# First layer of a two-layer kernel: decays and a norm factor spread over partitions by a trip through DRAM in place of transposes on TensorE

## The chip, the cores and the metric

The kernel runs on one core of a Trainium2 chip. The metric is the device time of one execution in microseconds (us); lower is better. The core has TensorE (PE in the profile, with PEld for its weight loads), VectorE (DVE), ScalarE (ACT), GpSimd (POOL) and SyncE (SP), which issues the DMAs here; SPq is SP's queue.

## What is computed

The input is 16 sequences of 512 tokens with 128 features. Both layers normalise the input, run two branches on it and add both to the residual. Cut to the part that the change touches, layer 0 is:

```
xn     = (x - mean) / sqrt(var + 1e-5)                  # layer norm, all tokens
# branch 1: a gated linear recurrence
xi, z  = split(xn @ W_in)
proj   = xi @ W_xp
delta  = softplus(proj[..., :1])                         # one number for each token
B, C   = proj[..., 1:65] @ W_B,  proj[..., 65:] @ W_C
A_bar  = exp(-exp(A_log) * delta)                        # one decay for each token, the same for all 256 channels
h_t    = A_bar_t * h_(t-1) + (B * xi)_t                  # scan over the tokens of a sequence
y      = ((C * h + D * xi) * silu(z)) @ W_out
# branch 2: eight experts, the best one for each token
top1   = argmax(xn @ Wg.T)
xhat   = layernorm(xn)                                   # a second norm, of xn
y2     = W2[top1] @ gelu(W1[top1] @ (xhat * scale + bias) + b1) + b2
x      = x + y + y2
```

Layer 1 is an attention of 16 heads with decays and level weights over dyadic segments of each sequence, plus a gated cell that runs over the 16 sequences one after another (the state of sequence b feeds sequence b + 1).

## The kernel before

**Stages.** The loop over i from -2 to 18 is layer 0, one sequence (called a batch below) for each step, with its stages spread over neighbouring steps: `norm0_stats(i+2)`, `norm0(i+2)` and `route(i+2)`, then `step_size(i+1)`, `decay_rows(i+1)` and `route2(i+1)`, then `mixers(i)`, `residual(i-1)`, `hand_over(i-2)` and `cell_step(i-3)`. The second loop, over 17 steps, is layer 1: `states`, `gates`, `diagonal`, `products`, `upper`, `upper2`, `diagonal2`, `finish`. The first layer-1 batch starts inside the last steps of layer 0. Layer 0 hands its result to layer 1 through DRAM tiles (`d_xt`, `d_xf`, `d_xh`, `d_xl`, and `d_x1`, which the profile shows as `d_x`).

**What sets the order.** No operation goes to the chip where it stands in the code. The class `Plan` records each with its dependences (`record`), prices it (`_price`), and `flush` lists all of them again, engine by engine: at each step the engine that is free earliest takes, among the operations whose inputs are ready by the planner's own clock, the one with the smallest key. The key is the time at which the operation must run for what follows it, plus a random number between -50 and 50 ns (`JIT`, seeded with `SEED`). On TensorE the planner also stays on a bank or on a tile shape where it can, and charges a time for a change of shape (`began += 100.0`). Each engine then runs its list strictly in that order, SyncE with its DMAs too. `record` also decides which earlier operations one depends on: those whose region of a tile it overlaps.

**The tiles that the change touches.** Tokens are laid out as 4 groups of 128 partitions (a column tile of 128 x 4 holds one number for each token). Channel-major work has 128 channels on the partitions and 512 tokens along the row. Two of the per-token numbers are needed channel-major, that is as a row of 512 repeated on all 128 partitions:
- `ab`, the decay, made in `step_size` and needed as `abr` by the two scans of `mixers`;
- `v2`, the factor of the second norm, made in `norm0_stats` and needed in `route` for `xq`, the experts' input.

Before, `spread(col, name)` does this by TensorE: four transposes of 128 x 128, each of one column broadcast along the row, into a PSUM bank. The bank is `par` for the decay, which ScalarE then copies into `abr`; it is `v2r` for the norm factor, which VectorE reads straight out of PSUM in the product `xq = v2r * xr`. `xr` is the transposed `xn`, copied from its bank `pxn` by ScalarE. `split` then makes the two halves `xnh` (rounded) and `xnl` (the rest) for products in three passes; both run on VectorE.

**Names in the profile.** Layer-0 tiles live in memory lent by layer-1 tiles, and the profile shows the lender: `xnh` and `xnl` are `lent_dec_xnh`, `xr` is `lent_ldr_xr`, `abr` is `lent_R_abr` (which also stands for one of the `ge` buffers), `xq` lies in `Gs`, the scans' outputs `hs` in `th_all`, `Gs` and `lent_vbd_x`, and `v2` appears as `v`. All operations carry the line of the statement that issues them, so tiles, not lines, tell them apart.

Of the kernel before, what the change touches and what calls it, by code (L numbers as in the profile page):

```python
# [12 lines left out]
F32 = mybir.dt.float32  # L13
# [3 lines left out]
ALU = mybir.AluOpType  # L17
AX = mybir.AxisListType
PSUM = bass.MemoryType.PSUM
# [3 lines left out]
T = 512  # L23
P = 128
NG = 4
# [21 lines left out]
KEPT = {"tr": 1, "pj": 2, "po": 1, "pg": 1}  # L47
MOST = {"tr": 3, "pj": 4, "po": 2, "pg": 3}

JIT, SEED = 50.0, 4  # L50


BLOCK, FIRST, ASK, LAND, HURRY = 254.25, 192.5, 1400.0, 2450.0, 2.0
# [2 lines left out]
class Plan:  # L56
# [52 lines left out]
    def record(self, eng, name, args, kw):  # L109
        op = Op()  # L110
        op.idx, op.eng, op.name, op.args, op.kw, op.base = len(self.ops), eng, name, args, kw, self.base
        op.deps, op.succ, op.fills, op.uses, op.inst, op.due = set(), [], [], set(), None, 0.0
        op.port = False
        i = op.idx
        aps = [(a, n == 0) for n, a in enumerate(args) if isinstance(a, bass.AP)]
        aps += [(a, False) for a in kw.values() if isinstance(a, bass.AP)]
        for ap, writes in aps:
            t, lo, hi, m = self._region(ap)
            past = self.seen.setdefault(t, [])
            if t in self.ring:  # L120
                op.uses.add(t)
                if not past:
                    op.fills.append(t)
                    self.first[t] = i
                elif self.first[t] != i:
                    op.deps.add(self.first[t])
            keep = []
            for rec in past:
                j, wrote, l, h, q = rec
                hit = l < hi and lo < h and q & m  # L130
                if hit and (writes or wrote) and j != i:
                    op.deps.add(j)
                if not (writes and hit and lo <= l and h <= hi and q | m == m and j != i):
                    keep.append(rec)
            keep.append((i, writes, lo, hi, m))
            self.seen[t] = keep
        if eng == "tensor":
            t = args[0].tensor.name
            if t in self.last_product:
                op.deps.add(self.last_product[t])  # L140
            self.last_product[t] = i
        self._price(op)
        self.ops.append(op)
        return i
# [101 lines left out]
    def flush(self):  # L246
# [79 lines left out]
        while len(order) < len(ops):  # L326
# [13 lines left out]
            while soon[e] and soon[e][0][0] <= now:  # L340
                _, key, i = heapq.heappop(soon[e])
# [5 lines left out]
            if e == "tensor":  # L347

                ahead = HURRY * max(0.0, fetched - now - (BLOCK - count) * 4.2)
                c = min(
                    able,
                    key=lambda c: (
                        c[0] > 1e8 or (
                            strips[ops[c[1]].kw["tile_position"][0] // 32] > strip + 60.0
                            if self._shape(ops[c[1]]) == shape == 2 else ops[c[1]].args[0].tensor.name != bank
                        ),
                        c[0] + 1000.0 * (self._shape(ops[c[1]]) != shape)  # L360
                        + ahead * (self._cols(ops[c[1]].args[0]) <= 64), c,
                    ),
                )
                can[e].remove(c)
                heapq.heapify(can[e])
                o = ops[c[1]]
                for k, n in place.get(o.idx, ()):
                    if not k[0]:
                        banks.pop(0)
                        taken[k] += 1  # L370
                        has[k[1]] += 1
                bank = o.args[0].tensor.name
                w = self._weights(o)
                began = max(now, max(began, o.fed) + (0.0 if w == held else w[2]))
                held = w

                at = max(o.kw["tile_position"]) // 32 if "tile_position" in o.kw else None
                if self._shape(o) != shape:
                    shape = self._shape(o)
                    strips = [0.0] * 4  # L380
                    began += 100.0
                if at is None:
                    strips = [0.0] * 4
                elif any(strips):
                    began = max(o.fed, strip + 17.0, strips[at])

                count += 4 if o.name == "matmul" and o.args[1].dtype == F32 else 2
                if count >= BLOCK:
                    count -= BLOCK
                    began = max(began, fetched)  # L390
                    fetched = max(began + ASK, moved) + LAND

                k = int((began + 100.0) / self.WINDOW)
                warm = columns.get(k - 1, 0.0) >= 3060.0
                o.end = max(began + o.dur * (1.0 if warm else 2.0), now + (22.5 if at is None else 14.5))
                rows = min(P, o.args[1].shape[0])
                part = 1.0 if at is None else 0.25
                columns[k] = columns.get(k, 0.0) + o.dur / 0.4167 * rows / P * part
                if at is not None:
                    strip, strips[at] = began, o.end  # L400
                free[e] = o.end + 2.5
            else:
                c = can[e][0]
                if e == "vector" and pool_end > now:
                    c = min(can[e], key=lambda c: c[0] + ops[c[1]].port * (pool_end - now))
                can[e].remove(c)
                heapq.heapify(can[e])
                o = ops[c[1]]

                if e == "gpsimd":  # L410
                    o.end = pool_end = max(now, port_end) + o.dur
                elif o.port:
                    o.end = port_end = max(now, pool_end) + o.dur
                else:
                    o.end = now + o.dur
                free[e] = o.end
# [40 lines left out]
def two_layer_kernel(ctx: ExitStack, tc: tile.TileContext, a: dict, out: bass.AP):  # L457
# [14 lines left out]
    def bank(name, tag="tr", shape=(P, 512), dt=F32):  # L472
        return nc.bank(ps, shape, dt, tag, name)
# [63 lines left out]
            nc.tensor.transpose(pt[:, g * P : (g + 1) * P], src[:, g, :], ident)  # L537
        return pt

    def spread(col, name):  # L540

        pr = bank(name)
        for g in range(NG):
            nc.tensor.transpose(pr[:, g * P : (g + 1) * P], col[:, g : g + 1].to_broadcast([P, P]), ident)
        return pr


    def handed(name, shape):
# [31 lines left out]
    for u, tag, dt in (  # L580
        ("c2h", "aY", F32R), ("c2l", "aY", F32R), ("xn", "bv", F32), ("c2", "yT", F32), ("tg0", "x1b", F32),
        ("tg1", "ysum", F32), ("x1s", "l0_x1s", F32), ("xr", "ldr", F32),
    ):
        lend(tag, 1, dt, [u])
    for u in ("tg2", "c2"):
        ring.setdefault(u, []).append(bt([P, 1, T], F32, "o", "lent_o_" + u, 2)[:, 0, :])

# [67 lines left out]
    for e in range(8):  # L655
        j = e % 4
# [85 lines left out]
    def norm0_stats(b):  # L742
        n, d = namer(b), S[b]
        xt = d["xt"]
        mv = norm_stats(xt, "la", n)
        rstd = norm_rstd(mv, "la", n)

        v2 = st([P, NG], F32, "v2", n("v2"))
        nc.vector.tensor_tensor(v2, rstd, rstd, op=ALU.mult)
        nc.vector.tensor_tensor(v2, v2, mv[:, :, 1], op=ALU.mult)  # L750
        act(v2, v2, AF.Ln, bias=eps_c)
        act(v2, v2, AF.Exp, scale=-0.5)
        d["norm"] = mv, rstd
        d["v2"] = v2

    def norm0(b):
        n, d = namer(b), S[b]
# [5 lines left out]
    def route(b):  # L763
        n, d = namer(b), S[b]
        pxn = transpose4(d["xn"], n("pxn"))
        xnh = st([P, T], F32R, "xnh", n("xnh"), 3)
        xnl = st([P, T], F32R, "xnl", n("xnl"), 3)
        xr = st([P, T], F32, "xr", n("xr"), 1)
        nc.scalar.copy(xr, pxn)
        split(xnh, xnl, xr)  # L770
        d["xn2"] = (xnh, xnl)
        d["xq"] = xq = st([P, T], F32, "xq", n("xq"))
        nc.vector.tensor_tensor(xq, spread(d["v2"], n("v2r")), xr, op=ALU.mult)

        plg = bank(n("plg"))
        for g in range(NG):
            nc.tensor.matmul(
                plg[32 * g : 32 * g + 32, :P], wlg, xr[:, g * P : (g + 1) * P],
                start=True, stop=True, tile_position=(0, 32 * g),
            )  # L780
        lgs = st([P, P], F32, "lgs", n("lgs"))
        nc.scalar.copy(lgs, plg[:, :P])
        plt = bank(n("plt"))
        nc.tensor.transpose(plt[:, :P], lgs, ident)
        d["lt"] = lt = st([P, NG, 9], F32, "lt", n("lt"))
        nc.vector.tensor_copy(lt, plt[:, :P].rearrange("p (g c) -> p g c", c=32)[:, :, 0:9])
# [37 lines left out]
    def decay_rows(b):  # L824
        n, d = namer(b), S[b]
        d["abr"] = abr = st([P, T], F32, "abr", n("abr"))
        nc.scalar.copy(abr, spread(d["ab"], n("par")))

    def mixers(b):
        n, d = namer(b), S[b]  # L830
# [627 lines left out]
```

## Time and profile before

| | us |
|---|---|
| median of 3 runs | 862.9 (862.58 to 863.74) |
| the profiled execution's own time | 864.26 |
| its span in the profile | 862.4 |
| TensorE (PE) busy | 811.3 (94%) |
| VectorE (DVE) busy | 727.0 (84%) |
| ScalarE (ACT) busy | 630.9 (73%) |
| GpSimd (POOL) busy | 302.7 (35%) |

The span runs from the first to the last instruction; the profiled execution's own time is 1.9 us more. A busy share is the time in which at least one instruction of that engine was in flight, so products that overlap in TensorE's pipeline count once, and the share says nothing of how close the engine is to its rate; the distance from one start to the next does. In a line of the timeline the first two numbers are the start and the duration, in us, of what may be several equal instructions (x4), and a bracket at its end gives the time for which the engine stood idle before it and what ended that. In a group line, the numbers behind the first bar are the busy time of the group in us and the mean of one in ns; behind the second bar is the idle time before it. Line L443 is the planner's single statement that issues everything.

### The profile page before, as it was taken

To read this page: it belongs to the slowest core of one execution; us is meant where nothing else is said; L and a number is where in the kernel's file an instruction comes from. 1 tells how busy PE (TensorE), PEld (TensorE's weight loads), DVE (VectorE), ACT (ScalarE), POOL (GpSimd) and SP (SyncE) were. 2 spreads that over 40 slices of the span, in tenths; PEclk is the share of its full clock that TensorE was granted. 3 is DMA by queue.
4 is the path that set the end of the run, shared out by engine and by line. 5 is a ranking of instruction groups with operands and counts; after the bars stand their busy time and mean duration, and the time that the engine had idled before them with its cause. 6 is when DMAs were issued, how large, how long until landed. Compare 5 with 4: busy or idle time off the path is not lost.

```text
span 862.4 us, 27939 instructions
## 1 busy us (share of the span) xinstructions
PE 811.3 (94%) x11544; PEld 624.6 (72%) x11544; DVE 727.0 (84%) x1841; ACT 630.9 (73%) x1306; POOL 302.7 (35%) x300
## 2 busy tenths in 40 slices
PE   7999999999999888998999999999999999999972
PEld 3778777778778666776787787767777777777752
DVE  5999999999999687668888888878889889888485
ACT  5898889788795777774785786686696687688643
POOL 3423434333434362223225234324333423423311
PEclk8999999999999898999999999999999999999996
DMA  8315223122221234244255345445355344435312
GB/s 211 81 67 170 98 87 111 62 86 74 86 86 62 74 95 154 70 101 114 76 153 138 109 124 139 112 95 151 100 131 143 110 128 121 129 100 136 73 35 62
DMA packets 87539, 91.72 MB, mean 106 GB/s; under 512 B 25893, under 2 KB 63021, under 8 KB 85293
## 3 DMA queue, kind: packets, MB, share of 16 engines
q1 hardware_dynamic: 87412, 89.95, 36.7%
q8 instruction: 90, 1.47, 0.7%
q14 instruction: 37, 0.30, 0.1%
HBM read 55.31 MB, written 34.60 MB: 104 GB/s over the span
## 4 chain that ended last, share of the span: by engine, by line
PE 75%; DVE 10%; ACT 7%; issue 3%; DMA 2%; POOL 1%; SPq 1%; ACTq 0%; DVEq 0%; POOLq 0%
PE b_pT L443 16%; PE pg L443 8%; PE po L443 7%; PE b_pS L443 6%; PE b_pU L443 6%; PE pm L443 4%; PE b_pp L443 3%; PE pC L443 2%; PE pz L443 2%; PE pB L443 2%; PE pxi L443 2%; PE b_pY L443 2%; PE b_pG L443 2%; ACT th_all L443 2%; DVE b_dec L443 2%
## 5 line engine op out<-in xcount | busy, mean ns | idle before, releaser
L443 ACT COPY th_all<-b_pT 128x512 f32<-128x512 f32 x256 | 144.2, 612 | 42.3 <-PE b_pT L443 32.5
L443 PE MATMUL b_pT<-b_xh,A_h 128*128 128x512 f32 x256 | 109.0, 426 | 0.0
L443 PE MATMUL b_pT<-b_xh,A_l 128*128 128x512 f32 x256 | 101.8, 398 | 0.0
L443 PE MATMUL b_pT<-b_xl,A_h 128*128 128x512 f32 x256 | 100.9, 394 | 0.5 <-issue 0.5
L443 ACT ACT_TABLE_LOAD x71 | 91.1, 1283 | 2.0 <-PEq L1448 0.7
L443 DVE TENSOR_TENSOR_SCAN b_dec<-b_dd,upat 128x512 f32<-128x512 f32 x64 | 77.4, 1217 | 4.5 <-PE b_pyd L443 4.3
L443 POOL TENSOR_TENSOR b_u<-b_u,b_vz 128x704 f32<-128x704 f32 x16 | 27.7, 1728 | 151.8 <-DVE b_vz L443 55.7
L443 PEld LDWEIGHTS b_pU<-th_all,Gs 128*32 128x32 f32 x4096 | 62.6, 112 | 21.6 <-issue 10.1
L443 PE MATMUL b_pU<-th_all,Gs 128*32 128x64 f32 x4096 | 71.5, 223 | 4.1 <-DVE Gs L443 2.4
L443 PE MATMUL b_pS<-th_all,b_xf 128*32 128x512 f32 x512 | 59.8, 594 | 1.0 <-DVE b_dec L443 1.0
L443 PEld LDWEIGHTS b_pT<-b_xh,A_l 128*128 128x128 f32 x256 | 48.4, 189 | 12.2 <-issue 0.7
L443 DVE TENSOR_TENSOR b_dec<-b_dec,b_pl 128x512 f32<-128x512 f32 x64 | 40.1, 681 | 19.6 <-PE b_pl L443 19.5
L443 PEld LDWEIGHTS b_pT<-b_xh,A_h 128*128 128x128 f32 x256 | 48.5, 189 | 11.0 <-DVE b_tiles L443 0.3
L443 PEld LDWEIGHTS b_pT<-b_xl,A_h 128*128 128x128 f32 x256 | 48.7, 190 | 7.6
L443 ACT COPY b_yq<-b_pU 128x512 f32<-128x512 f32 x64 | 37.1, 601 | 20.4 <-PE b_pU L443 19.8
L443 DVE TENSOR_TENSOR b_dec<-b_pS,b_dec 128x512 f32<-128x512 f32 x64 | 43.5, 682 | 1.6 <-PE b_pS L443 1.3
L443 DVE TENSOR_TENSOR b_aY<-b_pY,b_la 128x384 f32<-128x384 f32 (+2 forms) x64 | 34.3, 542 | 11.1 <-PE b_pY L443 7.8
L443 POOL TENSOR_TENSOR b_o<-b_o,rows 128x512 f32<-128x512 f32 x15 | 19.5, 1301 | 55.8 <-ACT b_o L443 55.8
L443 POOL TENSOR_TENSOR b_ysum<-b_aY 128x128 f32<-128x128 f32 x60 | 30.0, 505 | 25.5 <-DVE b_aY L443 25.2
L443 PE MATMUL pg<-lent_yq_x1h,lent_hh_w 128*128 128x512 f32 x96 | 34.5, 434 | 4.3 <-DVE lent_yq_x1h L443 2.1
L443 POOL TENSOR_TENSOR b_ld<-b_ldr,b_ld 96x512 bf16<-96x512 f32 x16 | 19.5, 1217 | 52.0 <-DVE b_ld L443 44.3
L443 POOL TENSOR_TENSOR b_x<-b_x,b_hh 128x512 f32<-128x512 f32 x16 | 20.6, 1290 | 44.2 <-DMA b_x<-d_x 25.5
(269 smaller groups left out, 2316.0 us busy)
## 6 DMA issues: line engine op xcount, KB each, us to landing
b_dd<-b_dde SPq DMA_DIRECT2D x64, 256.0 KB, 5.7
b_dld<-b_ld SPq DMA_DIRECT2D x48, 96.0 KB, 3.7
b_R<-b_dld SPq DMA_DIRECT2D x16, 288.0 KB
d_x<-lent_l_x1s_x1s SPq DMA_DIRECT2D x16, 256.0 KB, 3.1
d_xt<-lent_vbd_x SPq DMA_DIRECT2D x16, 256.0 KB
d_xf<-th_all SPq DMA_DIRECT2D x16, 256.0 KB, 2.0
b_xt<-d_xt SPq DMA_DIRECT2D x16, 256.0 KB, 4.0
d_xh<-lent_yq_x1h SPq DMA_DIRECT2D x16, 256.0 KB, 2.3
```

The costliest lines, as they stand in the source:

```text
L443: o.inst = getattr(getattr(self.nc, o.eng), o.name)(*o.args, **o.kw)
```

## The change

- `spread` no longer uses TensorE. It writes the column (128 x 4) to a DRAM row of 512 numbers, token by token, and reads that row back broadcast to 128 partitions, both by DMAs that SyncE issues. The DRAM rows share one ring of four buffers.
- `abr` is filled by that DMA; ScalarE's copy of it is gone. It has a second buffer, lent by `ld3`.
- The norm factor lands in a new tile `v2r`, with two buffers lent by `u` and `sp`; the spread is asked for in `norm0_stats`. `xq` is now the product of that tile and of the bank `pxn` (before: of the bank `v2r` and of `xr`).
- `xnh` is made by ScalarE, not by VectorE.
- In the planner: an operation of any engine but TensorE that reads a PSUM bank depends on every product recorded into that bank so far, not only on those that it overlaps; a change into a tiled shape is priced at 200 ns, not 100; the seed of the random part of the keys is 7, not 4.

```diff
-JIT, SEED = 50.0, 4
+JIT, SEED = 50.0, 7
...
                 hit = l < hi and lo < h and q & m
-                if hit and (writes or wrote) and j != i:
+
+                full = ap.space == PSUM and eng != "tensor" and wrote
+                if (hit and (writes or wrote) or full) and j != i:
                     op.deps.add(j)
...
                 if self._shape(o) != shape:
                     shape = self._shape(o)
                     strips = [0.0] * 4
-                    began += 100.0
+                    began += 200.0 if shape else 100.0
...
-    def spread(col, name):
-
-        pr = bank(name)
-        for g in range(NG):
-            nc.tensor.transpose(pr[:, g * P : (g + 1) * P], col[:, g : g + 1].to_broadcast([P, P]), ident)
-        return pr
+    def spread(dst, col, name):
+
+        row = nc.tile(dram, [T], F32, "row", name, 4)
+        nc.sync.dma_start(row.rearrange("(g p) -> p g", p=P), col)
+        nc.sync.dma_start(dst, row.partition_broadcast(P))
...
+    for tag, u in (("ld3", "abr"), ("u", "v2r"), ("sp", "v2r")):
+        lend(tag, 1, F32, [u])
...
-        d["v2"] = v2
+        d["v2r"] = v2r = st([P, T], F32, "v2r", n("v2r"))
+        spread(v2r, v2, n("v2d"))
...
-        split(xnh, xnl, xr)
+        split(xnh, xnl, xr, hi=nc.scalar)
...
-        nc.vector.tensor_tensor(xq, spread(d["v2"], n("v2r")), xr, op=ALU.mult)
+        nc.vector.tensor_tensor(xq, d["v2r"], pxn, op=ALU.mult)
...
-        nc.scalar.copy(abr, spread(d["ab"], n("par")))
+        spread(abr, d["ab"], n("abd"))
```

## The prediction

> **What bounds the kernel now.** I read the busy time in windows first: it says which engine sets the pace in which stage. Columns: window, its length, then the busy time of PE, PEld, DVE, ACT and POOL (with instructions), the granted clock, the DMA share and GB/s.
>
> ```profile
> 140.00:180.00 40.00, 40.00 (x258) 32.43 (x256) 38.72 (x94) 33.08 (x77) 15.43 (x12) 1.00 0.23 80
> 260.00:300.00 40.00, 35.91 (x198) 28.57 (x197) 31.98 (x71) 25.95 (x52) 13.96 (x10) 0.91 0.20 72
> 460.00:500.00 40.00, 39.36 (x768) 29.83 (x760) 34.70 (x94) 26.62 (x54) 16.08 (x20) 1.00 0.46 121
> ```
>
> In layer 0 (first line; every window from 60 to 260 us is like it) PE never stops and DVE rests 4%. At the hand-over to layer 1 (second line) both fall back and the granted clock sinks to 0.91. Layer 1 (third line) is PE's again. The change edits layer 0, so its worth is read from the first two.
>
> A busy PE need not be at its rate, so I read the timeline for start-to-start distances in the steady state.
>
> ```profile
> 140.17 0.60 PE L443 MATMUL v2r<-pk,v 128*128 128x128 f32 x4
> 140.70 0.43 PE L443 MATMUL plg<-lent_ldr_xr,wlg 128*32 128x128 f32 x8
> ...
> 155.54 0.60 PE L443 MATMUL par<-pk,ab 128*128 128x128 f32 x4
> 155.98 0.39 PE L443 MATMUL poh<-identb,oh 128*128 128x128 bf16 x4
> ```
>
> Four transposes hold PE for 155.98 - 155.54 = 0.44 us (0.53 for v2r, but 0.09 of that is the change to the tiled `plg`, which stays). No gap stands before or behind them. One batch takes 18.4 us: the first group of `pm` products starts at 134.48 and again at 152.84.
>
> Then the groups with their mean durations, for what moves between DVE and ACT:
>
> ```profile
> L443 DVE CAST lent_dec_xnh<-lent_ldr_xr 128x512 fp32r<-128x512 f32 x16 | 9.7, 608 | 0.2 <-ACT lent_ldr_xr L443 0.2
> L443 ACT COPY lent_R_abr<-par 128x512 f32<-128x512 f32 x16 | 9.4, 586 | 0.0
> L443 ACT CAST lent_aY_c2h<-lent_o_c 128x512 fp32r<-128x512 f32 x8 | 5.0, 619 | 2.1 <-DVE v L443 2.1
> ```
>
> **Part by part: steady layer 0.** PE loses 2 groups of transposes for each of 16 batches: 32 x 0.44 = 14.1 us, all where PE is saturated. That is the upper bound. DVE loses the cast, 608 ns a batch; `xq` stays one product of a PSUM and an SBUF operand (685 ns in the groups). So PE would need 18.37 - 0.88 = 17.5 us a batch. DVE's mean over the five windows from 60 to 260 us is 38.4 of 40, 96%, which is 17.6 us a batch, and 17.0 without the cast. It would have to be 97% busy to keep up with PE. If it rests 4% as now, a batch takes 17.0 / 0.96 = 17.7, and the gain is 0.63 x 16 = 10 us. I take 10, because DVE's present waits are for ACT, POOL and PE results that are not sped up; 14 and 6 (DVE resting 5.5%) are the ends. ACT swaps the 586 ns copy for a cast of about 619: 16 x 0.03 = 0.5 us, with ACT busy 33 of 40, so on no path; without that cover it would cost those 0.5 us.
>
> **The trips through DRAM.** Each batch gets four more DMAs on SP, none of which the trace of before shows. The nearest issues (KB each, median us to landing):
>
> ```profile
> b_dde<-b_ldr SPq DMA_DIRECT2D x16, 32.0 KB, 2.6
> b_dld<-b_ld SPq DMA_DIRECT2D x48, 96.0 KB, 3.7
> b_dd<-b_dde SPq DMA_DIRECT2D x64, 256.0 KB, 5.7
> ```
>
> The column out is 2 KB in 4-byte pieces; the broadcast back is 256 KB, the same kind as `b_dd`, four of which leave together, while a lone 256 KB load `th_all<-in_x` takes 3.0. So a round trip costs 2.6 + 3.0 = 5.6 to 3.7 + 5.7 = 9.4 us; I take 7, since one broadcast is nearer to the lone load. The Trainium skill speaks against this part: "DMA: Bandwidth & Descriptors", Rules for kernel authors, has a strided last dimension lowered to one descriptor for each element, which here means 512 descriptors for 2 KB. No row of before has such a store.
>
> What hides the trip is the time from the factor to its reader. In the timeline the decay of one batch is ready at 147.15 and its first scan starts at 162.14: 15 us, and 10.4 in the tightest steady batch. The norm factor has 10 to 19 us before `xq`. So it costs nothing while a trip stays under 10 us; beyond that every us is one on DVE, for each batch. On SP four issues at 0.3 to 0.5 us are under 2 us of 17.7. But SP is in order: the reload waits for its own store to land (2.6 to 3.7 us), and behind it stand the stores of `d_x`, `d_xt`, `d_xf`, `d_xh`, `d_xl` and the next input load. Their buffers come up again a batch later, so some 4 to 7 us of delay is covered. `xq` now holds the bank `pxn` until the factor has landed; the banks `par` and `v2r` are gone in exchange.
>
> **Start.** Here there is no slack.
>
> ```profile
> 22.80 0.28 ACT L443 ACTIVATE ab<-ab,row 128x4 f32<-128x4 f32 x1
> ...
> 24.86 1.22 DVE L443 TENSOR_TENSOR_SCAN th_all<-lent_R_abr,th_all 128x512 f32<-128x512 f32 x1
> ...
> 12.93 5.95 DMA pk<-in_pk
> ```
>
> The first scan follows its decay by 1.8 us, and a load in the first 20 us takes 6 us to land (third line, from the chain of waits). In the order of the changed kernel the first decay's store and reload stand on SP behind the 576 KB of `sell`, two norm rows and one input load, and DVE runs both first `xq` products ahead of the first scan. A trip of 5.6 to 9.4 from 23.1 puts the scan at 29 to 32.5, 4 to 7.5 us late. Before, `pm` of batch 0 starts at 27.5, 2.6 behind the scan, and needs the banks that the scans free. PE has in its place three groups of `pa` (2.05 us for two, so 3.1) moved ahead, and three transpose groups fewer (-1.9 by their starts). `pm` can go at 31.6 to 35, PE is there at 27.5 + 3.1 - 1.9 = 28.7: a stall of 3 to 6, taken as 4, with up to 1 us more from a sunk clock.
>
> **Hand-over.** Here PE waits on the chain that the transposes belong to:
>
> ```profile
> 282.20 0.43 PE L443 MATMUL plg<-lent_ldr_xr,wlg 128*32 128x128 f32 x8 [0.56 <-DVE Gs L443]
> 283.01 0.33 PE L443 MATMUL plt<-pk,lgs 128*128 128x128 f32 x1 [0.39 <-ACT lgs L443]
> 283.63 0.66 PE L443 MATMUL px<-pk,lent_vbd_x 128*128 128x128 f32 x4 [0.29 <-DVE lt L443]
> 285.15 0.65 PE L443 MATMUL par<-pk,ab 128*128 128x128 f32 x4 [0.87 <-ACT ab L443]
> 287.79 0.59 PE L443 MATMUL pm<-ohT,wmask 128*128 128x512 bf16 x1 [1.98 <-DVE lent_dd_th L443]
> ```
>
> The brackets sum to 4.1 us, and the `b_pp` products behind run at 0.36 us a start for 4 us where 0.20 is usual: another 2. In the changed order `plg` of the last batch stands ahead of 20 `po` products and `plt` ahead of six product groups and three gates, so this chain is covered. I take 4 of the 6; the ends are 6 and 0 (what is late next is the cell's chain of `pg` products, which stops PE 2.1 us at 336 and 2.0 us at 340 now).
>
> **Layer 1.** Its work is the same; the seed and the two planner edits deal its order anew. PE's idle time in the windows from 340 to 820 sums to 13 us, so a new deal can win no more than that. I take 0, with 4 either way.
>
> **Sum.** -10 + 4 - 4 + 0 = -10 us. The profiled execution's 864.26 becomes 854.3; it lies 1.4 above the median, so 862.9 becomes 853.
>
> **Rivals.**
> - *The trip becomes the bound* (slower). Place: both scans of each batch wait for `abr`. It decides from a trip of 10 us in the tightest batches and 15 in the others. For it: 4-byte pieces without any row, and reloads queued behind waiting stores. Against: 9.4 even by the slow rows. At 17 us a batch waits about 2 us more than it does now: 15 x 2 = 30, less the 14 of PE, plus 4 at the start, makes 883; with 10 to 12 us only early batches wait, and it lands near 866. Chance 0.13.
> - *DVE stays the bound.* Stalls of DVE take back the 0.6 us a batch; what is left is the start (+4) against the hand-over (-4): 863. For it: DVE at 96%; against: the cast comes off the same engine. Chance 0.08.
> - *The change does little itself, the deal decides.* Layer 1 and the hand-over lose 8 by new stalls while layer 0 gains 6 and the start costs 4: 869. Against: the products for a layer-1 batch stand in nearly the same order in both lists. Chance 0.07.
> - The forecast keeps 0.72, with 846 to 862 as its own range.
>
> **From cases to numbers.** 0.2%, or 1.7 us, is what a measurement can tell from no change. The forecast's 0.72 counts as faster. The DVE case splits 0.03 faster, 0.03 same, 0.02 slower; the deal 0.02 faster, 0.02 same, 0.03 slower; the trip is slower throughout. Faster 0.77, same 0.05, slower 0.18. The lower end takes 14, 3 and 6 with 0 for layer 1: 862.9 - 17 = 846. The upper end reaches into the trip's mild form: 866.
>
> **What would show it.** Right: no `par` or `v2r` on PE; `pm` starts about 17.7 us apart; the first scan at 29 to 32 us with PE idle for about 4 us ahead of the first `pm`; no scan that waits for a DMA later on; the brackets at the hand-over gone. Wrong: DVE idle with a DMA onto `lent_R_abr` or `lent_ld_abr` named in most batches, a store of the column that lands later than 5 us, or a pitch of 18.4 us as before.

## The result, and the profile after

The changed kernel takes 923.4 us (median of 4 runs, 921.8 to 927.0) against 863.2 before in the same series: 1.070 of the time before, 95% interval 1.067 to 1.074. The forecast was 853, with 846 to 866 as its range. The profiled execution took 924.63 us with a span of 922.3.

The busy time in windows, first the start, then the three windows shown of before (window, length, busy PE, PEld, DVE, ACT, POOL, granted clock, DMA share, GB/s):

```profile
20.00:60.00 40.00, 16.72 (x67) 11.99 (x66) 13.46 (x38) 10.71 (x25) 6.99 (x8) 0.59 0.43 69
140.00:180.00 40.00, 35.50 (x201) 27.29 (x200) 28.88 (x67) 28.48 (x63) 14.11 (x10) 0.91 0.78 99
260.00:300.00 40.00, 39.39 (x246) 30.28 (x245) 37.34 (x100) 33.95 (x76) 14.80 (x11) 1.00 0.40 108
460.00:500.00 40.00, 39.40 (x804) 28.93 (x792) 34.29 (x90) 26.62 (x53) 14.21 (x15) 1.00 0.39 106
```

The first of these windows before:

```profile
20.00:60.00 40.00, 38.93 (x257) 30.27 (x256) 36.50 (x104) 34.07 (x83) 13.69 (x12) 1.00 0.22 63
```

At the start PE works 17 us of 40 (before 38.9), and its granted clock sinks to 0.59. In 140 to 180 us PE and DVE both rest, though DVE was 97% busy there before. In layer 1 (last line) nothing is amiss. Milestones in the timeline place the loss: the first `pm` starts at 57.2 instead of 27.5 us (+29.7), the first `b_pG` of layer 1 at 413.4 instead of 345.5 (+67.9), and the span ends at 922.3 instead of 862.4 (+59.9). So the start loses 30 us, the rest of layer 0 another 38, and layer 1 wins back 8.

The waits of DVE and of SP's queue in the first 360 us say on what (total, times, longest):

```profile
DVE Gs L445 <- DMA lent_sp_v2r<-v2d: 25.8, 4, 11.0
DVE Gs L445 <- DMA lent_u_v2r<-v2d: 22.7, 4, 9.0
DVE lent_vbd_x L445 <- DMA lent_ld_abr<-abd: 19.5, 4, 9.6
DVE th_all L445 <- DMA lent_R_abr<-abd: 13.2, 4, 9.0
DVE v L445 <- DMA v2d<-v: 7.5, 1, 7.5
SPq L445 <- DMA v2d<-v: 100.3, 16, 9.6
SPq L445 <- DMA abd<-ab: 69.1, 11, 11.8
```

DVE waits for the reloads in 16 places, four of them on each buffer, for 81 us. On SP 27 reloads wait for the store of their own column, 6.3 us each on average (169 us in all). Two of the signs that the prediction named for being wrong are here: DVE idle with a DMA onto the decay's buffers named (ahead of the first scan of 8 batches up to 360 us, and of 9 of the 16 in all), and column stores that land later than 5 us. The timeline of SP shows one such store by itself, with nothing else issued around it:

```profile
54.82 0.38 SPq L445 DMA_DIRECT2D abd<-ab  x1
63.49 0.33 SPq L445 DMA_DIRECT2D lent_ld_abr<-abd  x1
```

2 KB need 8.7 us to land, where the prediction took 2.6 to 3.7. And at the start (SP's issues, then DVE with its waits in brackets):

```profile
17.78 0.38 SPq L445 DMA_DIRECT2D v2d<-v  x1
...
26.77 0.33 SPq L445 DMA_DIRECT2D lent_u_v2r<-v2d  x1
27.61 0.37 SPq L445 DMA_DIRECT2D abd<-ab  x1
28.28 1.09 SPq L445 DMA_DIRECT2D v2d<-v  x1
```
```profile
39.23 0.69 DVE L445 TENSOR_TENSOR Gs<-lent_u_v2r,pxn 128x512 f32<-128x512 f32 x1 [8.98 <-DMA lent_u_v2r<-v2d]
...
49.81 0.69 DVE L445 TENSOR_TENSOR Gs<-lent_sp_v2r,pxn 128x512 f32<-128x512 f32 x1 [9.30 <-DMA lent_sp_v2r<-v2d]
...
53.18 1.22 DVE L445 TENSOR_TENSOR_SCAN th_all<-lent_R_abr,th_all 128x512 f32<-128x512 f32 x1 [0.24 <-DMA lent_R_abr<-abd]
```

The first norm factor is under way from 17.8 to 39.2, 21.5 us; the store takes 9.0 of them, but the reload, a plain 256 KB broadcast, takes 12.5; the column store of the next batch went out 1.5 us ahead of it (25.23), two more stand right behind. The store also holds its source: DVE's 7.5 us for `v2d<-v` in the list above end at 26.77, when it writes the column tile `v` again, and the first decay is finished only after that. The first decay needs 25.6 us, from 27.61 to its scan at 53.18. Three theories could explain such times, and the runs below were chosen to part them.

### The profile page after: what moved, and what is told of

Same layout as the page of the kernel before. It is cut to its first block, busy times and chain, and to the rows that moved or that the text cites. A ratio compares the mean times of both kernels' runs of the same rounds, so it can differ in the third digit from the quotient of the medians.

```text
span 922.3 us, 27860 instructions
## 1 busy us (share of the span) xinstructions
PE 814.9 (88%) x11416; PEld 616.8 (67%) x11416; DVE 708.9 (77%) x1825; ACT 626.0 (68%) x1306; POOL 298.0 (32%) x300
## 4 chain that ended last, share of the span: by engine, by line
PE 39%; DVE 12%; ACT 7%; DMA 5%; issue 4%; POOL 2%; SPq 0%; ACTq 0%; DVEq 0%; POOLq 0%
PE b_pT L445 13%; PE b_pU L445 5%; PE b_pS L445 4%; DVE b_dec L445 3%; PE b_pY L445 2%; DMA abd<-ab 2%; ACT th_all L445 2%; PE b_pe L445 2%; PE b_pp L445 2%; PE b_po L445 2%; PE b_pG L445 1%; PE po L445 1%; PE b_pl L445 1%; DVE b_o L445 1%; PE b_pyd L445 1%
## 5 line engine op out<-in xcount | busy, mean ns | idle before, releaser
L445 ACT COPY th_all<-b_pT 128x512 f32<-128x512 f32 x256 | 146.7, 630 | 23.5 <-PE b_pT L445 19.6
L445 PEld LDWEIGHTS b_pT<-b_xh,A_l 128*128 128x128 f32 x256 | 48.0, 188 | 11.3
L445 POOL TENSOR_TENSOR lent_l_x1s_x1s<-lent_vbd_x,rows 128x512 f32<-128x512 f32 x16 | 22.7, 1416 | 90.0 <-DVE sc L445 73.4
L445 ACT COPY b_yq<-b_pU 128x512 f32<-128x512 f32 x64 | 38.5, 620 | 11.3 <-PE b_pU L445 11.0
L445 PE MATMUL pg<-lent_yq_x1h,lent_hh_w 128*128 128x512 f32 x96 | 34.7, 438 | 12.2 <-DVE Gs L445 10.5
L445 DVE TENSOR_TENSOR b_aY<-b_pY,b_la 128x384 f32<-128x384 f32 (+1 forms) x64 | 34.3, 548 | 11.4 <-PE b_pY L445 5.9
L445 PE MATMUL pC<-lent_dec_xnh,lent_vbd_w 128*128 128x512 f32 x96 | 31.8, 444 | 10.5 <-DVE Gs L445 10.5
L445 PE MATMUL pxi<-lent_dec_xnh,lent_vbd_w 128*128 128x512 f32 x96 | 31.5, 436 | 8.5 <-DVE lt L445 8.3
```

The lines of the kernel that those rows point to most:

```text
L445: o.inst = getattr(getattr(self.nc, o.eng), o.name)(*o.args, **o.kw)
```

## The experiments

Theory A: the store in 4-byte pieces is slow and holds back what is queued behind it. B: the planner's new order is at fault. C: any trip through DRAM is too long. Kernels of a series ran beside the kernel before, whose medians were 862.5, 862.8 and 861.8 us in the three series.

**Transposes back on TensorE, all other edits kept (e1_pe_spread).**

```diff
...
-        nc.sync.dma_start(row.rearrange("(g p) -> p g", p=P), col)
-        nc.sync.dma_start(dst, row.partition_broadcast(P))
...
+        for g in range(NG):
+            nc.tensor.transpose(pr[:, g * P : (g + 1) * P], col[:, g : g + 1].to_broadcast([P, P]), ident)
...
```

> The changed kernel with the four transposes for each spread back on TensorE (abr copied by ScalarE, xq = v2r bank times xr); the cast of xnh on ScalarE, the wider dependence of bank readers, the price of 200 and seed 7 stay. Theory A (the store of the column in 4-byte pieces lands about 9 us late and holds back what is queued behind it): near the kernel before or a little under, 852 to 864 us, since layer 1 alone ran 6 to 8 us shorter in the trace of the changed kernel. Theory B (the new order of the planner is at fault, the trips only show where it hurts): 900 us or more.

Measured: 855.0 us, ratio 0.991 (0.988 to 0.994). Without the trip, the planner's edits, the seed and `xnh` on ScalarE do no harm; together they bring 7.5 us. So B does not explain the loss: the changed kernel with its trips is 68 us above this one.

**The trip alone, in the kernel before (e2_dram_only).** The same two DMAs, lent buffers and product `xq` put into the kernel before, nothing else changed.

> The kernel before with the spread through DRAM alone (second buffer of abr, v2r tile, xq from pxn); xnh on VectorE, old dependences, price 100 and seed 4 stay. A: 915 to 935 us, the loss of the changed kernel without its gain in layer 1. B: 850 to 870 us. Theory C (any round trip through DRAM is too long here, whatever the pieces) gives 915 to 935 as well.

Measured: 910.1 us, ratio 1.057 (1.052 to 1.062), a few us better than theory A had it. In its waits up to 360 us DVE stands before the same tiles under the old order:

```profile
DVE lent_vbd_x L443 <- DMA lent_ld_abr<-abd: 31.2, 4, 12.7
DVE th_all L443 <- DMA lent_R_abr<-abd: 15.1, 3, 9.8
```

The trip costs 48 us here (910.1 against 862.5) and 68 in the new order (923.4 against 855.0), so the two parts of the change do not add: the order that wins 7.5 us without the trip loses 13 with it. Why was not tried.

**Pieces of 16 bytes (e3_16_bytes).** The four numbers of a partition go out side by side.

```diff
-        nc.sync.dma_start(row.rearrange("(g p) -> p g", p=P), col)
+        nc.sync.dma_start(row.rearrange("(p g) -> p g", g=NG), col)
```

> The changed kernel with the column stored in the order (partition, group): 128 pieces of 16 bytes in place of 512 of 4 bytes; decays and factors then reach the tokens in a permuted order, so values are wrong while work and waits are the same. A: the store lands in 3 to 5 us, VectorE's waits for the two reloads fall from 82 us to under 30, 865 to 890 us. C: within 5 us of the changed kernel's 923. B: 923 too.

Measured: 845.1 us, ratio 0.980 (0.978 to 0.983), better than theory A had it. One line of layout is worth 78 us. By the two traces all five engines run the same instructions in the same order as in the changed kernel, apart from the form of the store, so the planner's order has no part in it. Its DMA issues (count, KB each, median us to landing) and a window:

```profile
v2d<-v SPq DMA_DIRECT2D x16, 2.0 KB, 1.6
abd<-ab SPq DMA_DIRECT2D x16, 2.0 KB, 2.5
lent_u_v2r<-v2d SPq DMA_DIRECT2D x8, 256.0 KB, 5.3
lent_sp_v2r<-v2d SPq DMA_DIRECT2D x8, 256.0 KB, 3.6
```
```profile
140.00:180.00 40.00, 39.90 (x248) 30.59 (x246) 39.26 (x105) 35.88 (x78) 15.53 (x12) 1.00 0.38 117
```

Store and reload are now 5 to 7 us, the price that the prediction had taken, and PE and DVE are both full. C falls too.

**Four pieces of 512 bytes (e4_512_bytes).** One transpose of the whole column, a copy by ScalarE, and a store of four rows.

```diff
+        nc.tensor.transpose(pr[:NG, :P], col, ident)
...
+        nc.scalar.copy(r4, pr[:NG, :P])
...
+        nc.sync.dma_start(row, r4)
...
```

> The changed kernel with the column first turned by one transpose on TensorE into four rows of 128, copied by ScalarE, and stored in four pieces of 512 bytes; the broadcast reload is unchanged. A: the store lands in 2 to 3 us, steady batches run near 17.7 us, the start still loses some us: 845 to 862 us. C: 900 us or more, as the reload and the second landing remain. B: over 900.

Measured: 854.3 us, ratio 0.992 (0.988 to 0.996). The stores are quick (up to 360 us SP waits 0.9 us on average for one to land), but DVE now waits 11 times, 11.6 us in all, for the transposed bank of the routing (`lt` on `plt`; 1.0 us in the 16-byte kernel), and the trip has two steps more. What it loses against the 16-byte form was not followed further.

**What is it about 4-byte pieces? A chain of stores on an idle machine (e6_probe).** Appended behind the end of the kernel before; in the timeline each store is followed by a small read of it, whose issue marks the landing.

> The kernel before, with a chain of transfers behind its last instruction, on a machine that is otherwise idle; the results of the kernel are as before, and the time of the chain is read from the distances of SP's issues. Three turns of six stores, each read back by a small load that the next one waits for: 4 pieces of 512 B, 512 pieces of 4 B, 128 pieces of 16 B, 512 pieces of 4 B that lie 512 B apart, 128 pieces of 16 B that lie 512 B apart, 128 pieces of 512 B. Then four times a store that nobody reads with a load of 256 KB right behind it: 512 B, 4 B, 512 B, 4 B. Theory A (the count of pieces sets it): both stores of 512 pieces land about 8.7 us after their issue, those of 128 pieces and of 4 pieces within 2 to 4 us, and distance between pieces plays no part; the load behind a 4-byte store lands some 6 us later than behind a 512-byte one. Rival D (neighbouring 4-byte pieces collide in one line of DRAM): the store whose pieces lie 512 B apart is as quick as the 16-byte ones, 2 to 4 us. Rival E (the store is only slow beside the other traffic of the kernel): the lone 4-byte store lands in 3 to 4 us.

SP's issues in the second turn: 4-byte pieces side by side, 16-byte pieces, 4-byte pieces 512 B apart, each with its read:

```profile
890.39 0.39 SPq L443 DMA_DIRECT2D p<-probe  x1
899.52 0.24 SPq L443 DMA_DIRECT2D probe<-p  x1
901.67 0.34 SPq L443 DMA_DIRECT2D p<-probe  x1
903.48 0.24 SPq L443 DMA_DIRECT2D probe<-p  x1
905.52 0.39 SPq L443 DMA_DIRECT2D p<-probe  x1
907.30 0.24 SPq L443 DMA_DIRECT2D probe<-p  x1
```

9.1, 1.8 and 1.8 us (over three turns 8.3 to 9.4, 1.4 to 2.0, and 1.8 each time). So theory A as first put is wrong in one word: the number of pieces is not what costs. 512 pieces are as quick as 128, if they lie apart. Rival D's forecast came true (that the pieces meet in one line of DRAM is its picture, which no run here shows), and E falls, since the machine was idle. The busy share of the DMA engines (the number before the last) says where the time goes, first for the pieces side by side, then for those 512 B apart:

```profile
891.20:891.70 0.50, 0.00 (x0) 0.00 (x0) 0.00 (x0) 0.00 (x0) 0.00 (x0) 0.50 0.51 4
891.70:899.50 7.80, 0.00 (x0) 0.00 (x0) 0.00 (x0) 0.00 (x0) 0.00 (x0) 0.50 0.00 0
906.40:906.85 0.45, 0.00 (x0) 0.00 (x0) 0.00 (x0) 0.00 (x0) 0.00 (x0) 0.50 0.56 5
906.85:907.30 0.45, 0.00 (x0) 0.00 (x0) 0.00 (x0) 0.00 (x0) 0.00 (x0) 0.50 0.00 0
```

Both times the engines are done with all pieces within half a microsecond. Then nothing moves until the landing, for 7.8 us in one case and 0.45 in the other. The time does not go into handing out 512 pieces; it passes between the last piece and the landing. The last part of this probe says nothing: the load wrote the tile that the store was still reading, and so waited for it.

**At which distance? (e10_probe2)**

> The kernel before, with a second chain of transfers behind its last instruction; results as before, and the time of the chain is read from the distances of SP's issues. Two turns: 512 pieces of 4 B side by side; the same at distances of 8, 16, 32, 64 and 128 B; 128 pieces of 4 B side by side; 512 pieces of 4 B at 8 B, but with the four pieces of one partition next to each other. Then twice an unread store with a load of 256 KB into another tile right behind it, for 512 B pieces, 4-byte pieces side by side, 4-byte pieces 512 B apart. In the first chain the pieces side by side took 8.3 to 9.4 us, pieces 512 B apart 1.8. Theory D (pieces collide in a common line, so the time goes with how many share it): at 64 B or more 1.8 us, in between falling about in halves, 4.5 us at 8 B and 2.5 at 16; 128 pieces side by side, also 16 to a line, still take most of the 8 to 9 us if lines are served side by side, or a quarter, 2 to 3 us, if all collisions are served one by one. Theory F (a store is either merged or slow at another boundary): a step at one distance. The load behind the store: if a slow store holds its queue, it lands some 6 us later behind the pieces side by side; if not, as soon as behind the others, 2.7 to 3.1 us after its issue.

SP's issues in the second turn: 512 pieces side by side, at 8 B, at 32 B, then 128 pieces side by side, each with its read:

```profile
906.75 0.39 SPq L443 DMA_DIRECT2D p<-probe  x1
916.41 0.25 SPq L443 DMA_DIRECT2D probe<-p  x1
918.34 0.38 SPq L443 DMA_DIRECT2D p<-probe  x1
921.66 0.24 SPq L443 DMA_DIRECT2D probe<-p  x1
...
926.27 0.38 SPq L443 DMA_DIRECT2D p<-probe  x1
928.07 0.24 SPq L443 DMA_DIRECT2D probe<-p  x1
...
935.31 0.34 SPq L443 DMA_DIRECT2D p<-probe  x1
942.19 0.24 SPq L443 DMA_DIRECT2D probe<-p  x1
```

9.7 us side by side, 3.3 at 8 B, 2.2 at 16 B, and 1.8 at 32, 64 and 128 B. In the first turn, with a load issued behind each of these stores, it was 4.5 at 8 B, 3.0 at 16 B and 1.9 at most beyond. The order of the pieces matters little: at 8 B, with the four pieces of each partition next to each other, 3.3 us (3.7 in the first turn). A quarter of the pieces, but side by side, still takes 6.9 us (7.5 in the first turn). So the time goes with how close the pieces lie, as theory D had it, and much less with their number. The six loads of 256 KB do not stand where the run meant them: the planner moved them ahead, each behind a store of the first turn, so no load stands behind the unread stores. The first store of pieces side by side, the load behind it, and the first issue that waits for that load:

```profile
855.69 0.45 SPq L443 DMA_DIRECT2D p<-probe  x1
856.23 0.51 SPq L443 DMA_DIRECT2D probe<-in_x  x1
...
867.55 0.74 SPq L443 DMA_DIRECT2D p<-probe  x2
```

11.3 us; behind the stores at 8, 16, 32 and 64 B the same load took 5.1, 3.8, 2.9 and 2.9, behind the one at 128 B 3.1 (issued 888.05, its reader 891.13). The first also had a 256 KB store of the kernel's result 1 us ahead of it, and the others had not, so the next two runs ask the same inside the kernel.

**An unread store more, side by side or apart (e11_near_unread, e12_far_unread).** Both are the 16-byte kernel with one line more in `spread`; nobody reads `junk`, which has four buffers.

```diff
+        nc.sync.dma_start(junk.rearrange("(g p) -> p g", p=P), col)
```
```diff
+        nc.sync.dma_start(junk.rearrange("(g p) s -> p g s", p=P)[:, :, 0], col)
```

> The kernel with 16-byte stores (845.1 us; the values land permuted, which changes the numbers and not the work), with one more store ahead of each of its 32: the same column in 512 pieces of 4 B side by side, which nobody reads. SP pays 32 x 0.4 us for issuing it and has time. Theory G (a slow store holds back what is queued behind it): the reloads and the other transfers land late as in the changed kernel, 880 us or more. Theory H (a slow store costs only what waits for that store itself): nobody waits, so 843 to 853 us.

> The kernel with 16-byte stores (845.1 us; the values land permuted, which changes the numbers and not the work), with one more store ahead of each of its 32: the same column in 512 pieces of 4 B that lie 512 B apart, which nobody reads. Theory D (only pieces side by side are slow; pieces 512 B apart took 1.8 us on the idle machine): 843 to 853 us, whatever the run with pieces side by side gives. Theory A (the count of pieces is what hurts in the running kernel): as that run, within 5 us, and 880 us or more if a slow store holds back what is behind it.

Measured: 941.6 us side by side, ratio 1.092 (1.089 to 1.094); 852.9 us apart, ratio 0.990 (0.987 to 0.993). The same bytes, the same 512 pieces, and by the traces the same instructions in the same order on all five engines: 89 us between them, for a store that nobody reads. Few waits are put down to such a store itself (side by side: 7.0 us of DVE at the start, which may not write `v` again before, and 9.7 us of SP in three places), so most of the 89 us has to come from what stands behind it. Theory G holds and H falls. In the timeline of the first, the unread stores are the ones with a `j`:

```profile
97.90 0.43 SPq L445 DMA_DIRECT2D v2d_4j<-v  x1
98.44 0.44 SPq L445 DMA_DIRECT2D abd<-ab  x1
...
108.84 0.32 SPq L445 DMA_DIRECT2D lent_ld_abr<-abd  x1
```

The 16-byte store `abd`, which takes 2.5 us in the 16-byte kernel (median), lands 10.4 us after its issue, with `v2d_4j` ahead of it and one more unread store behind. From 105.0 to 108.5 us the DMA engines move nothing at all (share 0.00), as in the pause of the idle machine.

**Only one of the two columns by DRAM (e8_decay_only, e9_norm_only).** `spread_pe` is the old function; one of the two callers uses it again.

> The changed kernel with only the decay through DRAM in 4-byte pieces; the norm's factor is spread by TensorE again. Nothing that is computed changes. With both by TensorE it took 855 us, with both through DRAM 923. Theory A1 (a store holds the queue for 8.7 us; two fill a batch of 17.5 us, one does not): the single store nearly hides, a trip of 12 us against 10 to 15 us of slack, and the start loses some 10 us: 860 to 875 us. Theory A2 (each store costs what it is late by, whatever else is in the queue): about half of the 68 us stays, 885 to 895 us.

> The changed kernel with only the norm's factor through DRAM in 4-byte pieces; the decay is spread by TensorE again. Nothing that is computed changes. Theory A1 (two stores fill the queue, one does not): 858 to 872 us, since the factor has 10 to 19 us before its reader and only the start pays. Theory A2 (each store costs what it is late by): 880 to 895 us. If the losses of this run and of the one with the decay alone, both against 855 us, sum to well under 68 us, the two stores hinder each other.

Measured: decay alone 887.8 us, ratio 1.032 (1.027 to 1.036); norm factor alone 882.8, ratio 1.025 (1.021 to 1.029). Against the 855.0 with neither they lose 32.8 and 27.8 us, 60.6 together, and both at once lose 68.4. So the losses nearly add up: A2 is right here, and A1, a queue that overflows only with two stores, is wrong. A store costs time by itself, in two ways. The column's own reader waits: up to 360 us DVE stands 27.7 us for the reloads of the decay where that goes alone, and 35.2 us for those of the norm factor where that goes alone. And what stands behind is late: with the decay alone DVE waits 17.8 us for input loads (`la_st` on `th_all<-in_x`), against 3.4 in the kernel before. How the losses divide between the two was not parted. With the norm factor alone, the DMA issues show transfers that have nothing to do with the change:

```profile
th_all<-in_x SPq DMA_DIRECT2D x14, 256.0 KB, 6.9
d_x<-lent_l_x1s_x1s SPq DMA_DIRECT2D x16, 256.0 KB, 9.8
```

Before, the same two issues landed after 3.0 and 3.1 us.

**The planner told of the slow store (e5_planner_told).**

```diff
             op.dur = 475.0
+            if any(x.space == DRAM and x is a[0] and tuple(x.ap)[-1][0] == P for x in aps):
+                op.move = 7000.0
             return
```

> The changed kernel, with one line added to the planner's prices: the transfer of a store in 4-byte pieces is priced at 7 us, so that the list places the reload, its readers and what stands behind it on SP for a store that lands late. Nothing that is computed changes. Theory A1 (two such stores a batch hold the queue for some 2 x 8.7 = 17.4 us of each 17.5 us batch, so no order can hide them): 900 us or more. Theory A2 (the store is only late, and the list of the changed kernel was made for one that is not): the list gives it 7 us of lead and the time falls to about 865 us, with the DVE waits for the reloads below 20 us in all.

Measured: 914.7 us, ratio 1.062 (1.058 to 1.065). The number is A1's, but the last paragraph has shown A1 wrong, and A2's 865 is missed by 50. DVE's waits for the reloads do shrink to 3.5 us and SP's for the stores from 169 to 27, as A2 wanted, yet the time hardly moves. The price moves those who read the store; those who stand behind it still land late:

```profile
d_xt<-lent_vbd_x SPq DMA_DIRECT2D x16, 256.0 KB, 9.9
lent_u_v2r<-v2d SPq DMA_DIRECT2D x8, 256.0 KB, 13.9
abd<-ab SPq DMA_DIRECT2D x16, 2.0 KB, 14.1
```

With the unread stores apart, the first two land after 2.8 and 5.0 us. That the delay of such transfers accounts for all of the 914.7 is argued, not shown.

**A version below both kernels (e7_best).** The norm factor goes out in 16-byte pieces, and `xq` reads it in that order; the decay, whose scan needs its tokens in line, by one transpose, a copy and four pieces of 512 B; the first three norm factors and the first two decays by the old transposes, since the start has no slack.

```diff
...
+            nc.vector.tensor_tensor(
+                xq.rearrange("c (g p) -> c g p", g=NG), d["v2r"].rearrange("c (p g) -> c g p", g=NG), pxn.rearrange("c (g p) -> c g p", g=NG), op=ALU.mult
+            )
...
+        if b < 2:
+            nc.scalar.copy(abr, spread_pe(d["ab"], n("par")))
...
```

> The changed kernel with the quickest stores that keep its results: the norm's factor goes out in 16-byte pieces and is read by the product in the order in which it landed; the decay is turned by one transpose to four rows, copied by ScalarE and goes out in 4 pieces of 512 B; the first three norm factors and the first two decays are spread by TensorE as before, since the start has no slack. Nothing that is computed changes. Theory A (slow are 4-byte pieces alone, the trip itself is affordable): the steady layer keeps a pitch of 17.4 to 17.8 us, the start loses at most 4 us, 833 to 848 us, below both kernels. If the start cannot be bought back by TensorE: 845 to 855 us.

Measured: 843.5 us, ratio 0.978 (0.976 to 0.981). The first `pm` starts at 29.5 us, 2 later than before, and the first window is full:

```profile
20.00:60.00 40.00, 39.15 (x259) 30.38 (x258) 36.56 (x91) 33.67 (x81) 14.36 (x12) 1.00 0.29 77
```

Against the 16-byte kernel it is 10.5 us ahead at the first `pm` (29.5 against 40.0), but only 3.9 at the end of the span (839.1 against 843.0): from 200 to 256 us its batches come 18.8, 18.9 and 17.9 us apart, where the 16-byte kernel has 17.3 to 17.7, and the last one 21.4 us behind the one before it, not 18.8. Why was not tried.

## Why the prediction was wrong, point by point

- **The price of the trip: the step that failed.** 5.6 to 9.4 us was built from the rows `b_dde` (2.6) and `b_dld` (3.7) for the store. Neither row has small pieces, and the text said itself that no row of before had such a store. The reload was priced well: 3.0 to 5.7 us, against 3.6 and 5.3 in the 16-byte kernel. The store alone took 8.3 to 9.7 us on the idle machine, two to four times as much. Together with such a reload that makes 12 to 15 us (an estimate from these rows), above the 10 us up to which the prediction held the trip to be free; the first two of the changed kernel took 21.5 and 25.6. "The nearest row" was the nearest in bytes; what set the time was how the pieces lie in DRAM.
- **"4 to 7 us of delay is covered": the step that made it dear.** The text saw that the stores of `d_x`, `d_xt` and the next input stand behind, but took the delay to be SP's wait and to pass once for each reload. It is longer and of another kind: a transfer issued behind the store lands late even when SP waits for nothing (941.6 against 852.9 us for unread stores). One column costs 28 to 33 us by two things together: this lateness, and a trip that is longer than the 10 us which its own readers can hide at the tightest. The share of each was not measured.
- **Start: +4, measured +29.7.** Two causes. With 16-byte stores it is still +12.5: the first scan runs at 35.5, not at 29 to 32, since the first trips share the queue with the constants (the decay, stored at 21.97, is reloaded at 28.98, behind a reload that waited for another store). The other 17 us are the slow stores. The prediction had no term for one part of them: DVE could not write `v` again before its store had landed (7.5 us), so that the first decay went out at 27.61 and not at 21.97. With the first batches left to TensorE it is +2.0.
- **Steady layer 0: -10, measured about +38 up to layer 1.** The engine side of the sum was right and even careful. In the 16-byte kernel nine batches take from 104.5 to 261.5 us, 17.44 each, where before took 18.39 (97.5 to 263.0): -0.94 a batch, beyond the 0.63 that was taken and the 0.88 that was called the upper bound, and DVE is 98% busy in the window shown. In the changed kernel the few batches without a stall do the same: `pm` at 276.5, 293.8 and 311.3. So neither "DVE stays the bound" nor a wrong reading of PE played a part.
- **`xnh` by ScalarE** cost what was said: 616 ns a cast (estimate 619) for a copy of 586.

```profile
L445 ACT CAST lent_dec_xnh<-lent_ldr_xr 128x512 fp32r<-128x512 f32 x16 | 9.8, 616 | 0.0
```

- **Hand-over.** The brackets at `plg`, `plt` and `px` are gone in the 16-byte kernel, as forecast. In the changed kernel one of 6.4 us stands before `px` at 333.7 instead, late like all else. In the 16-byte kernel the lead over before grows from 9.8 us at the last batch's `pm` (297.2 against 307.0) to 13.4 at the first `b_pG`: 3.6, about the 4 that was taken.
- **Layer 1: 0 with 4 either way, measured -8.0** (first `b_pG` to the end: 508.9 against 516.9 us). 6.0 remain in the 16-byte kernel and 1.6 in the one with transposes. A new deal of the order was worth more than the 4 us that were allowed, and less than the 13 us of idle time that bounded it; no run took the seed apart from the edits.
- **The rival "the trip becomes the bound"** named the right mechanism and the right signs, at 0.13, but its worst case stopped at 883. It counted 2 us a batch for DVE and 4 at the start, and had no term for the other transfers. Its chance should have been larger: for a cost without any row, the upper end of 9.4 us was taken from rows of another form, and nothing in the trace spoke for it.
- **The rule that spoke against it.** One descriptor for each element was named in the prediction and priced at nothing. The runs agree that such a store is dear, but the count does not measure it: 512 elements at 32 B or more from each other took 1.8 us when nothing else ran, 128 elements side by side 6.9. The same page of the Trainium skill ("DMA: Bandwidth & Descriptors", Queues, rings and completion order) says that a transfer's completion mark lands only after every earlier write of that DMA engine, across its queues. The 10.4 us of a quick store behind a slow one agree with that; a second queue was not tried, so no run here shows the last part.

## What to carry to other kernels

Before a transpose or a copy is replaced by a trip through DRAM, look at the innermost run of the address pattern on the DRAM side: here 4-byte pieces next to each other cost about five times what the same pieces cost 32 B apart, or what the same bytes cost in 16-byte runs. Price a slow transfer for everything that is issued behind it on its queue, not only for its reader. And a stage without slack, such as the first batches, can keep the old way while the steady state takes the new one.

## What the runs showed of the hardware that was not expected

- Stores of 4-byte pieces from 128 partitions, behind the end of the kernel: 8.3 to 9.7 us for 512 pieces side by side, 3.3 to 4.5 at 8 B, 2.2 to 3.0 at 16 B (the larger figures with a load of 256 KB behind), 1.8 to 1.9 from 32 B to 512 B; 6.9 to 7.5 us for 128 pieces side by side; 1.4 to 2.0 for the 512 numbers in pieces of 16 B; 1.2 to 2.0 in four pieces of 512 B. The DMA engines are done with the pieces within half a microsecond either way; the difference lies between the last piece and the landing (7.8 us against 0.45). What in the memory path makes neighbours slow was not tried.
- A store that nobody reads delays what is queued behind it: 2 KB in 16-byte pieces took 10.4 us in place of 2.5, and 32 such stores made 89 us.
- A lower clock comes with the stalls: 0.59 in the first window, 0.91 in the second one shown, where before had 1.00 in both.
